# A two-layer attention kernel: new places in the queue of layer 1's epilogue, and own buffers for its last block

## The chip, the cores and the metric

The kernel runs on one core of a Trainium2 chip, in one launch. The metric is the device time of that launch in microseconds (us): from the first to the last instruction of the program. The kernel before takes 3108.49 us, the median of three runs that lie between 3106.8 and 3109.73 us. The profile and the trace quoted below are of one further execution whose span is 3106.2 us.

The core has five engines which run at the same time and wait for one another by semaphores. In the profile they are called PE (TensorE, the matrix multiplier), DVE (VectorE), ACT (ScalarE), POOL (GpSimd) and SP (SyncE, which here starts the DMA transfers). PEld is the loading of weights into PE, which overlaps its matmuls.

## The reference, cut to what matters

The input `x` is (4, 128, 64, 64): four images of 4096 positions with 128 channels, in float32. Two layers follow one another.

```python
# layer 0
x = x + L0_conv(gn(x), ...)          # group norm, q, k, v, gate; softmax attention of
                                     # 4096 x 4096 with 64 channels; gate; projection
# layer 1
t = to_tokens(x)
h = ln(t)                            # layer norm
q = h @ W
t = t + softmax(q @ q.T) @ h         # attention, 4096 x 4096, 128 channels
Wx = ln(t) @ Wf.T                    # inputs of a recurrence
Wx = batch_norm(Wx)                  # mean and variance over all 4 * 4096 tokens
y[s] = sigmoid(Wx[s] + y[s-1] @ V.T) # a recurrence along the 4096 tokens
out = from_tokens(t + y)
```

The batch norm is what makes the end of layer 1 matter: no step of the recurrence can start before the statistics of the very last block of the last image are known.

## The kernel before, as far as the change touches it

For each of the four images (`b`) the kernel runs `layer0` and then `layer1`. Each walks over eight blocks of 512 queries (`n`). Within a block the inner loop makes scores on PE, the exponential on ACT, sums or block transposes on DVE, and the weighted sum on PE again. One turn of this inner loop is called a *place* here. In every place at most one small closure is taken out of a queue: `pending` holds the epilogues of finished blocks, `ahead` the preparation of the next image. So the small steps lie between the large matmuls.

The queue in layer 0 (a place in each turn of the loop over `p`):

```python
        def nothing():
            pass
        ...
        def attention(score_mm, bias, scale, weigh, finish, need):
            ...
            for n in range(NB):
                for p in range(PAIRS):
                    ...                                   # scores (L215), exp (L217), acc (L224),
                                                          # weighted sums (L394)
                    if ahead:
                        ahead.popleft()()
                    elif pending and (p % 2 == 0 or len(pending) > 6):
                        pending.popleft()()
```

The epilogue of a block in layer 1. All four steps that use a PSUM bank take it from one pool that has a single buffer, `ps_m`; that pool also serves the preparation of the next image (`mp`, lines 326, 346 and 361).

```python
            def finish(n):
                ...
                t = work.tile([P, 4, NQ, 32], F32, tag="t", name="t1", bufs=2)
                h2 = work.tile([P, NQ, C], F32, tag="h2", name="h2")
                th = work.tile([P, QB], F32, tag="th", name="th")
                t1 = work.tile([P, NQ, C], F32, tag="og", name="t1b")
                nc.sync.dma_start(t, t_d[b, n])

                def tokens():
                    ...                                        # denominators
                    m = ps_m.tile([P, NQ, P], F32, tag="m", name="mt")
                    for j in range(NQ):
                        nc.tensor.transpose(m[:, j, :], oacc[:, n, bass.ts(j, P)], ident)  # L557
                    for j in range(NQ):
                        nc.vector.scalar_tensor_tensor(t1..., m..., rinv..., t...)         # L559
                    layernorm(quarters(t1), quarters(h2))      # DVE L267 L268, POOL L131 L132, DVE L271

                def result():
                    m = ps_m.tile([P, QB], F32, tag="m", name="mr")
                    ...                                        # 4 transposes of t1, L569
                    t2 = work.tile([P, QB], F32, tag="xb", name="t2")
                    nc.scalar.copy(t2, m)                      # L571
                    nc.sync.dma_start(t2_d[b, :, cs], t2)      # L572

                def turn():
                    m = ps_m.tile([P, QB], F32, tag="m", name="mh")
                    ...                                        # 4 transposes of h2, L577
                    nc.scalar.copy(th, m)                      # L578

                def inputs():
                    m = ps_m.tile([P, QB], F32, tag="m", name="mw")
                    nc.tensor.matmul(m, lhsT=wt["f"], rhs=th, start=True, stop=True)       # L582
                    nc.vector.bn_stats(bn_st[:, b * NB + n, :], m)                         # L583
                    ...                                        # copy to wxs, L586 (wx, L589)

                if b == B - 1 and n == 0:
                    pending.extend([tokens, turn, inputs, result])
                else:
                    pending.extend([tokens, result, turn, inputs])
```

In layer 1 a place takes from `pending` first and from `ahead` only when `pending` is empty:

```python
                        if pending:
                            pending.popleft()()
                        elif ahead:
                            ahead.popleft()()
```

The end of layer 1 and the start of the recurrence:

```python
        flush()                                    # what is left in pending
        ok = big.tile(...)                         # checks of the denominators
        ...
    with ExitStack() as st:
        scan = st.enter_context(tc.tile_pool(name="scan", bufs=1))
        ...
        banks = ...                                # six banks, each begun by one matmul, L725
        mv = scan.tile([P, 2], F32, name="bn_mv")
        nc.vector.bn_aggr(mv, bn_st...)            # L730
        gain = scan.tile([P, 1], F32, name="gain")
        inv_sqrt(gain, mv[:, 1:2], EPS_BN)         # POOL L131 L132
        ...                                        # gain and bias, L737
        preload(1); preload(2)                     # L751
        for k, i in enumerate(steps):              # 44 steps, in two halves each
            ...
                if k == 0:
                    nc.scalar.activation(dst, at(wxs, i, bs), AF.Sigmoid, ...)   # L761
                    continue
                nc.tensor.matmul(bank(k, s), lhsT=wt["vt"], rhs=before, ...)     # L764
                nc.scalar.activation(dst, bank(k, s), AF.Sigmoid, bias=bias)     # L768
```

The program that is run is not in the order of this text: each engine's instructions are put in order when the program is built. An engine then takes them one after the other.

Of the kernel before, what the change touches and what calls it, by code (L numbers as in the profile page):

```python
# [10 lines left out]
F32 = mybir.dt.float32  # L11
I32 = mybir.dt.int32
AF = mybir.ActivationFunctionType
# [5 lines left out]
P = 128  # L19
B, C, N = 4, 128, 4096  # L20
# [9 lines left out]
QB = 512  # L30
NB = N // QB
NQ = QB // P
# [125 lines left out]
def fast(  # L158
# [3 lines left out]
    nc = tc.nc  # L162
    keep_ctx = ExitStack()
    keep = keep_ctx.enter_context(tc.tile_pool(name="keep", bufs=1))
    bn_st = keep.tile([P, B * NB, 6], F32, name="bn_st")
    den_all = keep.tile([P, 2 * B * NT], F32, name="den_all")

    with ExitStack() as st:
        big = st.enter_context(tc.tile_pool(name="big", bufs=1))
        ep = st.enter_context(tc.tile_pool(name="ep", bufs=4))  # L170
        accp = st.enter_context(tc.tile_pool(name="accp", bufs=1))
        work = st.enter_context(tc.tile_pool(name="work", bufs=1))
        stat = st.enter_context(tc.tile_pool(name="stat", bufs=4))
        ps_s = st.enter_context(tc.tile_pool(name="ps_s", bufs=2, space=PSUM))
        ps_o = st.enter_context(tc.tile_pool(name="ps_o", bufs=3, space=PSUM))
        ps_m = st.enter_context(tc.tile_pool(name="ps_m", bufs=1, space=PSUM))
# [4 lines left out]
        pending: deque = deque()  # L181

        def nothing():
            pass

        done = set()

# [5 lines left out]
        def attention(score_mm, bias, scale, weigh, finish, need):  # L193


            fifo: deque = deque()
            o = None

            def pop():
                nonlocal o  # L200
                n, p, e, acc = fifo.popleft()
                if p == 0:
                    o = None
                o = weigh(o, n, p, e)
                if p == PAIRS - 1:
                    finish(n, o, acc)

            for n in range(NB):
                acc = first = None
                for p in range(PAIRS):  # L210
                    need(n, p)
                    ps = ps_s.tile([P, 2, QB], F32, tag="s", name="ps")
                    for h in range(2):
                        lhsT, rhs = score_mm(n, p, h)
                        nc.tensor.matmul(ps[:, h, :], lhsT=lhsT, rhs=rhs, start=True, stop=True)  # L215
                    e = ep.tile([P, 2, QB], F32, tag="e", name="e")
                    nc.scalar.activation(e, ps, AF.Exp, scale=scale)  # L217
                    if p == 0:
                        first = e
                    elif p == 1:  # L220
                        acc = accp.tile([P, 2, QB], F32, tag="acc", name="acc", bufs=2)
                        nc.vector.tensor_tensor(acc, first, e, ALU.add)
                    else:
                        nc.vector.tensor_tensor(acc, acc, e, ALU.add)  # L224
                    fifo.append((n, p, e, acc))
                    if len(fifo) > LAG:
                        pop()
                        if p == 0:
                            pop()
                    if ahead:  # L230
                        ahead.popleft()()
                    elif pending and (p % 2 == 0 or len(pending) > 6):
                        pending.popleft()()
            while fifo:
                pop()
# [25 lines left out]
        def layernorm(src, dst):  # L261

            mv = stat.tile([P, NQ, 2], F32, tag="mv", name="mv")
            rstd = stat.tile([P, NQ], F32, tag="rstd", name="rstd")
            for j in range(NQ):
                s6 = stat.tile([P, 6], F32, tag="s6", name="s6")
                nc.vector.bn_stats(s6, src[j])  # L267
                nc.vector.bn_aggr(mv[:, j, :], s6)  # L268
            inv_sqrt(rstd, mv[:, :, 1], EPS_LN)
            for j in range(NQ):  # L270
                nc.vector.tensor_scalar(  # L271
                    dst[j], src[j], mv[:, j, 0:1], rstd[:, j : j + 1],
                    ALU.subtract, ALU.mult,
                )
# [191 lines left out]
        def layer1(b, h, qt):  # L466
# [74 lines left out]
            def finish(n):  # L541
                cs = bass.ts(n, QB)
                rinv = stat.tile([P, NQ], F32, tag="rinv", name="rinv")
                t = work.tile([P, 4, NQ, 32], F32, tag="t", name="t1", bufs=2)
                h2 = work.tile([P, NQ, C], F32, tag="h2", name="h2")
                th = work.tile([P, QB], F32, tag="th", name="th")
                t1 = work.tile([P, NQ, C], F32, tag="og", name="t1b")
                nc.sync.dma_start(t, t_d[b, n])

                def tokens():  # L550
                    at = (B + b) * NT + n * NQ
                    den = den_all[:, at : at + NQ]
                    nc.vector.tensor_reduce(den, slots[:, bass.ts(n, NQ), :], AX.X, ALU.add)
                    nc.vector.reciprocal(rinv, den)
                    m = ps_m.tile([P, NQ, P], F32, tag="m", name="mt")
                    for j in range(NQ):
                        nc.tensor.transpose(m[:, j, :], oacc[:, n, bass.ts(j, P)], ident)  # L557
                    for j in range(NQ):
                        nc.vector.scalar_tensor_tensor(  # L559
                            t1[:, j, :].rearrange("q (p i) -> q p i", p=4),  # L560
                            m[:, j, :].rearrange("q (p i) -> q p i", p=4), rinv[:, j : j + 1],
                            t[:, :, j, :], ALU.mult, ALU.add,
                        )
                    layernorm(quarters(t1), quarters(h2))

                def result():
                    m = ps_m.tile([P, QB], F32, tag="m", name="mr")
                    for j in range(NQ):
                        nc.tensor.transpose(m[:, bass.ts(j, P)], t1[:, j, :], ident)  # L569
                    t2 = work.tile([P, QB], F32, tag="xb", name="t2")  # L570
                    nc.scalar.copy(t2, m)  # L571
                    nc.sync.dma_start(t2_d[b, :, cs], t2)  # L572

                def turn():
                    m = ps_m.tile([P, QB], F32, tag="m", name="mh")
                    for j in range(NQ):
                        nc.tensor.transpose(m[:, bass.ts(j, P)], h2[:, j, :], ident)  # L577
                    nc.scalar.copy(th, m)  # L578

                def inputs():  # L580
                    m = ps_m.tile([P, QB], F32, tag="m", name="mw")
                    nc.tensor.matmul(m, lhsT=wt["f"], rhs=th, start=True, stop=True)  # L582
                    nc.vector.bn_stats(bn_st[:, b * NB + n, :], m)  # L583
                    m = m.rearrange("p (g i s) -> p i g s", i=L // 2, s=2)
                    if b == B - 1:
                        nc.vector.tensor_copy(wxs[:, :, b, bass.ts(n, GB), :], m)  # L586
                    else:
                        wx = work.tile([P, L // 2, GB, 2], F32, tag="wx", name="wx")
                        nc.vector.tensor_copy(wx, m)  # L589
                        nc.sync.dma_start(wxs_d[b, :, :, bass.ts(n, GB), :], wx)  # L590

                if b == B - 1 and n == 0:
                    pending.extend([tokens, turn, inputs, result])
                else:
                    pending.extend([tokens, result, turn, inputs])


            for n in [NB - 2, NB - 1] + list(range(NB - 3, -1, -1)):
# [4 lines left out]
                for a in order(n):  # L603
# [4 lines left out]
                    for i in range(2):  # L608
                        ps = ps_s.tile([P, 2, QB], F32, tag="s", name="ps")
                        e = ep.tile([P, 2, QB], F32, tag="e", name="e")  # L610
# [68 lines left out]
        def need(n, p):  # L679

            if n == 0:
                while p // 4 > 0 and n_ahead - len(ahead) < 6 * (p // 4):
                    ahead.popleft()()

        for b in range(B):
            xg, q, k, v = parts0
# [13 lines left out]
                ahead.popleft()()  # L700
        flush()

        ok = big.tile([P, 2, 2 * B * NT], F32, tag="oacc", name="ok")
        nc.vector.tensor_scalar(ok[:, 0, :], den_all, DEN_LO, None, ALU.is_ge)
        nc.vector.tensor_scalar(ok[:, 1, :], den_all, DEN_HI, None, ALU.is_le)
# [3 lines left out]
    with ExitStack() as st:  # L709
        scan = st.enter_context(tc.tile_pool(name="scan", bufs=1))  # L710
        ps_r = st.enter_context(tc.tile_pool(name="ps_r", bufs=1, space=PSUM))
        t2 = scan.tile([P, B, N], F32, name="t2s")
# [10 lines left out]
        for s in range(2):  # L723
            for i in range(3):
# [1 line left out]
                    banks[s][i][:, : HB * G], lhsT=ident, rhs=wxs[:, 0, :HB, :, 0],  # L726
                    start=True, stop=True, skip_group_check=True,
                )
        mv = scan.tile([P, 2], F32, name="bn_mv")
        nc.vector.bn_aggr(mv, bn_st.rearrange("p a b -> p (a b)"))  # L730
        gain = scan.tile([P, 1], F32, name="gain")
        inv_sqrt(gain, mv[:, 1:2], EPS_BN)
        nc.vector.tensor_mul(gain, gain, col(GAMMA))

        bias = scan.tile([P, 1], F32, name="bias")
        nc.vector.tensor_mul(bias, mv[:, 0:1], gain)
        nc.vector.tensor_sub(bias, col(BETA), bias)  # L737

# [3 lines left out]
        def bank(k, s):  # L742
            return banks[s][k % 3][:, : HB * G].rearrange("p (b g) -> p b g", g=G)
# [12 lines left out]
        for k, i in enumerate(steps):  # L756
# [15 lines left out]
            if k >= W:  # L772
                todo.extend((i - 3, b) for b in range(B) if i % 4 == 3)
                for j in range(len(todo) if i == L - 1 else min(1, len(todo))):
                    i0, b = todo.popleft()
# [418 lines left out]
```

## Time and profile before

| what | before |
|---|---|
| median of the runs | 3108.49 us |
| span of the profiled execution | 3106.2 us |
| PE busy | 3018.6 us, 97% of the span |
| DVE busy | 1877.7 us, 60% |
| ACT busy | 1144.8 us, 37% |
| POOL busy | 144.5 us, 5% |
| mean granted PE clock | 0.993 |

The first table of the profile's page says how long each engine was busy. The list of waits says, for each pair of an instruction and the one that it waited for, how many us the waiting engine sat idle in total, how many times, and how long at most. The timeline gives instructions in order of time: start in us, duration in us, engine, line, operation, the tile written, an arrow to the tiles read, and in square brackets the idle time of that engine just before, with the instruction that ended it. A table by windows cuts the span into stretches and gives each engine's busy time in each. A float32 matmul of this kernel stands in the trace as two records.

### The profile page before, as it was taken

Reading aid. Unit: us, or ns where it says so; the run is one execution under the profiler, and the core shown is the slowest. Engines: PE = TensorE matmul, PEld = TensorE weight load, DVE = VectorE, ACT = ScalarE, POOL = GpSimd, SP = SyncE. Lnnn points to the kernel's source line nnn. Section 1 sums busy time; section 2 is a strip of 40 time slices with the busy share of each in tenths; the row PEclk is TensorE's granted clock in tenths of the full one; section 3 lists DMA queues with packets and bytes.
Section 4 is the critical chain, followed back from the end, with each engine's and each line's share of the span. In section 5 each row is a group of like instructions: output and inputs, shape, how many; then the busy total and the mean of one; then the engine's idle time right before and its main releaser. Section 6 shows DMA issues by size and latency. Waiting matters only on the chain.

```text
span 3106.2 us, 32252 instructions
## 1 busy us (share of the span) xinstructions
PE 3018.6 (97%) x10706; PEld 1362.3 (44%) x10706; DVE 1877.7 (60%) x3160; ACT 1144.8 (37%) x2018; POOL 144.5 (5%) x183
## 2 busy tenths in 40 slices
PE   7999999999999999999999999999999999999976
PEld 3444444444444444444444444444444444444432
DVE  6666656555666665655566666555566666455546
ACT  3444433333344443333334443333334444323324
POOL 0000000000000000000000000000000000000000
PEclk9999999999999999999999999999999999999988
DMA  1011143333111123334211114333321113443423
GB/s 51 28 55 55 55 111 88 91 89 92 46 55 55 55 78 93 90 89 97 73 52 55 50 43 116 88 91 93 91 56 55 49 44 121 114 104 88 98 98 157
DMA packets 233168, 241.14 MB, mean 78 GB/s; under 512 B 88480, under 2 KB 144288, under 8 KB 231968
## 3 DMA queue, kind: packets, MB, share of 16 engines
q1 hardware_dynamic: 231984, 238.18, 28.2%
q8 instruction: 88, 1.44, 0.2%
q10 hardware_dynamic: 1008, 0.79, 0.1%
q14 instruction: 88, 0.72, 0.1%
HBM read 65.80 MB, written 56.62 MB: 39 GB/s over the span
## 4 chain that ended last, share of the span: by engine, by line
PE 91%; DVE 4%; SPq 1%; POOL 1%; DMA 1%; issue 1%; ACT 0%; ACTq 0%; DVEq 0%; POOLq 0%
PE o L394 28%; PE ps L215 15%; PE ps L613 15%; PE o L501 14%; PE ot L514 12%; SPq L650 1%; PE m L243 1%; PE mw L582 1%; PE mq L487 1%; PE mp L326 1%; PE ps_r L764 1%; PE mh L577 1%; POOL rstd L132 1%; DVE t1b L559 1%; PE mp L361 1%; PE mp L346 1%
## 5 line engine op out<-in xcount | busy, mean ns | idle before, releaser
L394 PE MATMUL o<-e,nxt 64*128 64x512 f32 x4096 | 963.8, 589 | 0.0
L217 ACT ACTIVATE e<-ps 128x1024 f32<-128x1024 f32 x512 | 521.4, 1025 | 674.7 <-PE ps L215 657.5
L224 DVE TENSOR_TENSOR acc<-acc,e 128x1024 f32<-128x1024 f32 x448 | 547.6, 1222 | 236.4 <-ACT e L217 220.5
L619 ACT ACTIVATE e<-ps,shift 128x512 f32<-128x512 f32 x580 | 393.9, 684 | 749.8 <-PE ps L613 497.1
L394 PEld LDWEIGHTS o<-e,nxt 64*128 64x128 f32 x4096 | 399.0, 187 | 482.3 <-issue 474.5
L613 PE MATMUL ps<-qt 128*128 128x512 f32 x1160 | 547.8, 595 | 2.7 <-ACT qt L488 2.7
L501 PE MATMUL o<-e,h 128*128 128x512 f32 x1160 | 537.7, 592 | 0.0
L215 PE MATMUL ps<-nxt 64*128 64x512 f32 x2048 | 534.5, 596 | 1.2 <-DVE nxt L338 0.9
L514 PE MATMUL ot<-tt,h 128*128 128x512 f32 x888 | 399.8, 593 | 0.0
L624 DVE STREAM_TRANSPOSE dd<-e 128x512 f32<-128x512 f32 x444 | 286.5, 686 | 83.4 <-ACT e L619 73.1
L501 PEld LDWEIGHTS o<-e,h 128*128 128x128 f32 x1160 | 218.3, 191 | 260.7 <-issue 259.5
L613 PEld LDWEIGHTS ps<-qt 128*128 128x128 f32 x1160 | 213.4, 191 | 249.0 <-issue 224.2
L215 PEld LDWEIGHTS ps<-nxt 64*128 64x128 f32 x2048 | 194.5, 187 | 231.5 <-issue 158.8
L514 PEld LDWEIGHTS ot<-tt,h 128*128 128x128 f32 x888 | 167.9, 190 | 210.0 <-issue 205.7
L519 DVE TENSOR_REDUCE slots<-tt 128x4 f32<-128x2048 f32 x111 | 250.7, 2258 | 9.7 <-DMA tt<-dd 9.4
L528 DVE TENSOR_TENSOR oacc<-oacc,ot 128x512 f32<-128x512 f32 x87 | 59.3, 682 | 209.8 <-PE ot L514 209.8
L131 POOL TENSOR_SCALAR rstd<-mv 128x4 f32<-128x4 f32 x64 | 14.6, 228 | 2456.5 <-DVE mv L268 2456.5
L619 ACT ACTIVATION_READ_ACCUMULATOR e<-ps,shift 128x1 f32 x580 | 113.9, 196 | 0.0
L448 DVE SCALAR_TENSOR_TENSOR t<-yt,rinv,t 128x128 f32<-128x128 f32 x128 | 36.6, 347 | 71.5 <-DMA yt<-turn_d 71.4
L411 POOL TENSOR_SCALAR xb<-xb,bpc 128x512 f32<-128x512 f32 x32 | 57.4, 1793 | 318.0 <-DMA xb<-in_x_dram 289.3
L132 POOL TENSOR_TENSOR rstd<-rstd,mhalf 128x4 f32<-128x4 f32 x64 | 66.4, 1038 | 5.3
L271 DVE TENSOR_SCALAR h<-t,mv,rstd 128x128 f32<-128x128 f32 x128 | 35.7, 343 | 47.1 <-POOL rstd L132 47.1
(134 smaller groups left out, 1491.7 us busy)
## 6 DMA issues: line engine op xcount, KB each, us to landing
tt<-dd SPq DMA_DIRECT2D x1776, 64.0 KB, 2.0
turn_d<-d SPq DMA_DIRECT2D x96, 256.0 KB, 2.0
t_d<-t SPq DMA_DIRECT2D x64, 256.0 KB, 2.0
nxt<-in_x_dram SPq DMA_DIRECT2D x16, 512.0 KB, 5.5
xb<-in_x_dram SPq DMA_DIRECT2D x32, 256.0 KB, 2.9
t<-turn_d SPq DMA_DIRECT2D x128, 64.0 KB, 2.0
yt<-turn_d SPq DMA_DIRECT2D x128, 64.0 KB, 2.0
qt<-turn_d SPq DMA_DIRECT2D x128, 64.0 KB, 2.0
```

Of the source, the lines that this page charges most:

```text
L132: nc.gpsimd.tensor_tensor(dst, dst, mhalf[:, :n], ALU.pow)
L215: nc.tensor.matmul(ps[:, h, :], lhsT=lhsT, rhs=rhs, start=True, stop=True)
L217: nc.scalar.activation(e, ps, AF.Exp, scale=scale)
L224: nc.vector.tensor_tensor(acc, acc, e, ALU.add)
L394: nc.tensor.matmul(o[r], lhsT=v[rs, p + h * PAIRS, :], rhs=e[rs, h, :], start=(p == 0 and h == 0), stop=(p == PAIRS - 1 and h == 1),)
L501: nc.tensor.matmul(o, lhsT=h[:, NQ * a + 2 * i + half, :], rhs=e[:, half, :], start=(a == order(n)[0] and i == 0 and half == 0), stop=(a = ...
L514: nc.tensor.matmul(ot, lhsT=h[:, NQ * n + j, :], rhs=t[:, :, j, :, :].rearrange("q p k j -> q k p j"), start=(j == 0), stop=(j == NQ - 1),)
L519: nc.vector.tensor_reduce(slots[:, bass.ts(n, NQ), a], t.rearrange("q p b k j -> q b p (k j)"), AX.XY, ALU.add,)
L528: nc.vector.tensor_tensor(oacc[:, n, :], oacc[:, n, :], o, ALU.add)
L613: nc.tensor.matmul(ps[:, half, :], lhsT=qt[:, bass.ts(at, P)], rhs=qt[:, bass.ts(n, QB)], start=True, stop=True,)
L619: nc.scalar.activation(e[:, half, :], ps[:, half, :], AF.Exp, bias=shift, accum_out=slots[:, at, n : n + 1],)
L624: nc.vector.transpose(d.rearrange("q f b k j -> q k b f j")[:, 2 * i + half], e[:, half, :].rearrange("q (b f j) -> q b f j", b=NQ, f=NQ),)
```

## The change

The change has five parts, all of them about the place and the buffers of small steps; no arithmetic is added or left out, except for one activation on a single column.

1. In layer 1 two places called `nothing` come between `result` and `turn`, so that the layer norm of `tokens` has more time before PE needs it. In such a place one step of `ahead` is taken, if there is one. In the last image the blocks 1, 2 and 3 are without them.
2. In layer 0 the entries that `pending` held at the start are taken in every place rather than in every second one.
3. The last block of the last image takes its PSUM banks from the pool of the scores and its SBUF buffers from the pool of the exponentials; its `tokens` step goes to the front of the queue.
4. The statistics and the gain and bias of the batch norm move from the pool of the recurrence to one that lives from the start.
5. A Sigmoid on one column is written after the last block, to have that function's table loaded early.

```diff
+    mv = keep.tile([P, 2], F32, name="bn_mv")
+    gain = keep.tile([P, 1], F32, name="gain")
+    bias = keep.tile([P, 1], F32, name="bias")
+    first_y = keep.tile([P, 1], F32, name="first_y")
 ...
         def nothing():
-            pass
+            if ahead:
+                ahead.popleft()()
 ...
+            left = len(pending)
 ...
-                    elif pending and (p % 2 == 0 or len(pending) > 6):
+                    elif pending and (p % 2 == 0 or left > 0 or len(pending) > 6):
+                        left -= 1
                         pending.popleft()()
 ...
+                if b == B - 1 and n == 0:
+                    one, two = (ep.tile([P, 2, QB], F32, tag="e", name="last") for _ in range(2))
+                    h2, t1 = (one[:, r, :].rearrange("q (j c) -> q j c", j=NQ) for r in range(2))
+                    th, t2 = two[:, 0, :], two[:, 1, :]
+                    def bank():
+                        return ps_s.tile([P, 2, QB], F32, tag="s", name="ml")[:, 0, :]
+                else:
+                    ...                            # buffers as before, bank() from ps_m
 ...
                 if b == B - 1 and n == 0:
-                    pending.extend([tokens, turn, inputs, result])
+                    pending.appendleft(tokens)
+                    pending.extend([result, turn, inputs])
+                elif b == B - 1 and n < 4:
+                    pending.extend([tokens, result, turn, inputs])
                 else:
-                    pending.extend([tokens, result, turn, inputs])
+                    pending.extend([tokens, result, nothing, nothing, turn, inputs])
 ...
         flush()
+        nc.scalar.activation(first_y, shift, AF.Sigmoid)
 ...
-        mv = scan.tile([P, 2], F32, name="bn_mv")
-        gain = scan.tile([P, 1], F32, name="gain")
-        bias = scan.tile([P, 1], F32, name="bias")
```

## The prediction

> **What bounds the kernel now.** I read the first table of the page, then the list of PE's waits, then the timeline around these waits, and last the table by windows.
>
> ```profile
> PE 3018.6 (97%) x10706; PEld 1362.3 (44%) x10706; DVE 1877.7 (60%) x3160; ACT 1144.8 (37%) x2018; POOL 144.5 (5%) x183
> ```
>
> PE is busy for all but 88 us of the 3106.2. The change takes no matmul away, so it can only win from those 88 us and from the few places where PE runs at half its clock. That alone says that 2% (62 us) is out of reach. Where are the 88 us, and which of them does the change touch? The list of waits, PE's own (total us, times, longest):
>
> ```profile
> PE mh L577 <- DVE h L271: 15.7, 21, 4.4
> PE ps_r L764 <- ACT y L761: 7.8, 1, 7.8
> ...
> PE mh L577 <- ACT e L619: 2.8, 3, 1.0
> ...
> PE mp L346 <- DVE nxt L351: 2.4, 3, 0.8
> PE mp L326 <- DVE nxt L351: 2.4, 3, 0.8
> ```
>
> The reader is to see three kinds: `turn` waiting for the layer norm (`mh`), two projections of the next image waiting for their single bank (`mp`), and waits that occur once, around the start of the recurrence (`ps_r`). One of the 24 `mh` waits, the longest, belongs to the last kind. A usual one looks like this in the timeline:
>
> ```profile
> 652.79 1.12 DVE L559 SCALAR_TENSOR_TENSOR t1b<-mt,rinv,t 128x128 f32<-128x128 f32 x4
> ...
> 655.97 1.04 POOL L132 TENSOR_TENSOR rstd<-rstd,mhalf 128x4 f32<-128x4 f32 x1
> ...
> 657.04 1.11 DVE L271 TENSOR_SCALAR h<-t1b,mv,rstd 128x128 f32<-128x128 f32 x4 [1.47 <-POOL rstd L132]
> ...
> 657.53 0.75 PE L577 MATMUL mh<-ident,h 128*128 128x128 f32 x3 [0.65 <-DVE h L271]
> ```
>
> Four DVE steps, the statistics, a round trip to POOL and four more DVE steps take 5.4 us (652.79 to 658.15); PE comes 0.65 us early. And the end of layer 1:
>
> ```profile
> 2996.32 0.68 DVE L528 TENSOR_TENSOR oacc<-oacc,o 128x512 f32<-128x512 f32 x1
> ...
> 3001.45 0.66 PE L557 MATMUL mt<-ident,oacc 128*128 128x128 f32 x4
> ...
> 3006.01 1.11 DVE L271 TENSOR_SCALAR h<-t1b,mv,rstd 128x128 f32<-128x128 f32 x4 [0.58 <-POOL rstd L132]
> ...
> 3008.38 2.08 PE L582 MATMUL mw<-th,w 128*128 128x512 f32 x2 [0.73 <-ACT th L578]
> ...
> 3011.11 0.67 DVE L586 COPY wxs<-mw 128x512 f32<-128x512 f32 x1
> ...
> 3015.81 1.02 DVE L730 BATCH_NORM_AGGREGATE bn_mv<-bn_st 128x2 f32<-128x192 f32 x1 [4.03 <-DMA t_d<-t]
> ...
> 3018.81 1.28 ACT L761 ACT_TABLE_LOAD   x1 [5.24 <-DVE bias L737]
> ...
> 3020.77 15.27 PE L764 MATMUL ps_r<-y,w 128*128 128x256 f32 x44 [7.82 <-ACT y L761]
> ```
>
> The last sum is there at 2997.00, but its transposes start at 3001.45, behind the other block's three uses of the one bank. The batch statistics are there at 3011.19, but the aggregate starts at 3015.81: its tile lies where a buffer was whose DMA had to land first. From 2997.00 to the first matmul of the recurrence it takes 23.8 us. The table by windows (length, then PE, PEld, DVE, ACT, POOL busy, PE's clock, DMA):
>
> ```profile
> 2997.00:3020.00 23.00, 9.36 (x32) 5.14 (x32) 10.07 (x33) 2.95 (x4) 2.18 (x5) 0.72 0.20 67
> ```
>
> PE's mean clock here is 0.72; the trace's clock record has it at half from 3006.9 to 3024.0.
>
> **What the Trainium skill says.** "TensorE: Matmul & The Clock Gate", section "What's actually happening": PE falls to half rate after about one idle window of 3.4 us and comes back after one busy window. The trace agrees: PE sat idle for 4.39 us before 3006.50, the clock fell at 3006.9, and the two records of `mw`, 1.11 us in all a block earlier (at 2998.96), took 2.08. [...] "PSUM — Partial Sum Buffer", "Engine vs sequencer instructions": matmuls start in program order and the other engines' queues are first in, first out. The timeline agrees: PE starts nothing else while `mh` waits. So where an instruction stands in its engine's queue decides, and that is known from the built program before any run.
>
> **The change, part by part.**
>
> *Two empty places.* In the built order of the first three images, `mh` comes two to four score records (one or two score matmuls) later than before, with weighted sums besides, in the six blocks per image that still lie in layer 1; the place of `h` in DVE's queue is as before. In layer 0 PE did not wait for `mh`, so the other two blocks have nothing to win. Two score records alone are 2 x 0.43 = 0.86 us and the sums between them bring more, against waits of 0.39 to 0.95 us. So these waits go. Per image they are 0.39 + 0.65 + 0.65 + 0.39 + 0.65 + 0.95 = 3.67 us. A matmul record lasts 590 ns, yet in a stream the next starts after 429, so each stall also loses the overlap of 0.16: 3.67 + 6 x 0.16 = 4.63, times three is **13.9 us**. In the last image blocks 7 and 6 move in the order; 5, 4 and 2 do not. That is (0.39 + 0.65) + 2 x 0.16 = **1.4 us** won; 2.1 us of waits stay.
>
> *`nothing` takes a step of `ahead`.* This spreads the preparation of the next image. In the order before, once per later image, two value projections and one query/key projection stand back to back on the one bank; in the new order other matmuls are between. That removes both `mp` waits: (0.78 + 0.17) x 2 x 3 = **5.7 us**, where 0.17 is again the lost overlap (276 ns record, 112 step). Against it, in three places a gate projection now stands only one matmul (0.86 us) ahead of `mh` on the same bank, and ACT's 0.78 us read with some 0.2 us before it must fit between: I allow **1.0 us** lost in all.
>
> *Leftovers in every place of layer 0.* More entries are left over than before, six per block instead of four. In the windows of layer 0 DVE is busy 229 of 343 us and PE all of it, so DVE has room and PE's matmuls only change their place: **0**.
>
> *The last block.* Its `mt` can start at 2997.06 rather than 3001.45. Its layer norm meets one obstacle: in DVE's new order the `bn_stats` of block 1 stands ahead of the last aggregate of the last block, and waits for `mw` of block 1, which ended at 3000.07. So `bn_stats` runs until about 3000.7, and from the last aggregate to `h` it was 3006.01 - 3004.35 = 1.66 us: `h` at 3002.4. From `h` to `mw` as before, 2.37: 3004.75. `mw` at full clock 1.11: 3005.9. Statistics and copy, 1.3: 3007.2. The tile of the aggregate has its own place now, so it starts at once: 3007.2 against 3015.81, **8.6 us** earlier. If the clock falls all the same, `mw` takes its 2.08 and it is 7.6. With full clock the first two steps of the recurrence also take about 2.6 instead of 3.6 us, 1.0 more. The six matmuls that begin the banks, which stood in idle time, now come after that last copy: 12 x 0.227 = 2.7 us, twice that at half clock. From the copy to the first matmul of the recurrence there are about 5 us, so they cost nothing at full and 0.5 at half clock. So 7.1 to 9.6; I take **8.8**.
>
> *The early table.* In the built order this activation stands at the very start of ACT's queue, since it needs only a constant. The table for the recurrence is still loaded after the bias: nothing won of the 1.28. At the start there is one load more, and ACT sits idle 14.4 us before its first activation and 2.3 before its first exponential: **0**, give or take 1.
>
> Sum: 13.9 + 1.4 + 5.7 - 1.0 + 8.8 = 28.8 us. 3108.5 - 28.8 = 3079.7, so 3080.
>
> **Rivals.**
> 1. *The wait only moves.* `mh` could come later and meet another wait: for the bank, for ACT's copy, or for a later `h` if DVE is late. For it: one bank serves five kinds of steps. Against it: `h` keeps its place, and in layer 0 with its longer distance no `mh` waited. If the waits of the empty places came back in full, 3095.
> 2. *The leftovers crowd layer 0.* Steps with 4 us of DVE work next to 1.22 us per place could hold back DVE, then the four buffers of the exponentials, then PE. For it: a place of layer 0 lasts only 2.6 us. Against it: the old rule also took one in every place while more than six were left, and PE shows no wait there. A few us per image, 3085 to 3095.
> 3. *The end is bound elsewhere.* If the recurrence's first tile must wait for memory of the last block's buffers, as the aggregate had to, part of the 8.8 is given back. Against it: the result's copy and DMA now stand ahead of `turn`, and a DMA landed in about 2 us before. It would make 3083 to 3085.
>
> **Range and chances.** The waits found are nearly certain to be at hand and the order says that they are passed, so most of the risk is in small new waits (later) and in the clock (2 us either way). Range 3073 to 3091: the low end needs all parts at their best and some further waits of the 88 us gone, the high end is one rival half true. Faster by over 2% would need 62 us: 0.01. Slower by over 2%: 0.01.
>
> **What would show it.** Right: no `mh` waits on `h` in the first three images, three left in the last; no waits of `mp` for L351's counterpart in layer 1; the aggregate directly after the copy of the last inputs, some 10 us after the last sum; a table load still between bias and recurrence, and three loads in all. Wrong: new waits of PE in the first blocks of layer 0 or at `mh` for ACT, or an aggregate that waits for a DMA still.

## The result and the profile after

The changed kernel takes **3074.59 us** (median of four runs, 3073.29 to 3075.83) against 3107.64 in the same comparison: ratio 0.9893, 95% interval 0.9875 to 0.9910. That is 33.1 us, against 28.8 foretold. In the profiled executions the spans are 3106.2 and 3074.0 us.

The first table of the page, after:

```profile
PE 3009.1 (98%) x10706; PEld 1366.4 (44%) x10706; DVE 1878.9 (61%) x3160; ACT 1144.4 (37%) x2020; POOL 149.3 (5%) x183
```

The counts say that no matmul went away; ACT has two instructions more, the early Sigmoid and its table load. PE's busy time fell by 9.5 us although it does the same work. That fits what the profile counts as busy: in a stream the record of a matmul (590 ns) overlaps the next one (429 ns later), before a stall it does not, and a group that waits piece by piece counts as busy throughout.

The lines of the changed kernel are numbered otherwise: the last epilogue's steps are L579 (`mt`), L592 (`mr`), L601 (`mh`) and L606 (`mw`), the scores of layer 1 L640, those of layer 0 L223. The list of PE's waits after, in the parts that answer to those shown of before (total, times, longest):

```profile
PE ps L640 <- ACT qt L497: 2.7, 4, 0.7
PE ml L601 <- DVE last L280: 2.5, 1, 2.5
PE ps L223 <- ACT e L225: 2.2, 1, 2.2
PE m L601 <- DVE h L280: 2.1, 3, 0.8
```

The waits of the projections (`mp`) are gone, and of the waits for the layer norm three are left, 2.1 us, all in the last image. One is new: a score of layer 0 waits 2.2 us for ACT. The end in the timeline:

```profile
2973.29 0.68 DVE L537 TENSOR_TENSOR oacc<-oacc,o 128x512 f32<-128x512 f32 x1
...
2974.02 0.65 PE L579 MATMUL ml<-ident,oacc 128*128 128x128 f32 x4 [1.66 <-DVE oacc L537]
...
2979.26 1.11 DVE L280 TENSOR_SCALAR last<-last,mv,rstd 128x128 f32<-128x128 f32 x4 [0.90 <-POOL rstd L132]
...
2981.43 1.56 PE L606 MATMUL ml<-last,w 128*128 128x512 f32 x2 [0.68 <-ACT last L602]
...
2983.64 0.68 DVE L610 COPY wxs<-ml 128x512 f32<-128x512 f32 x1
2984.23 1.01 DVE L758 BATCH_NORM_AGGREGATE bn_mv<-bn_st 128x2 f32<-128x192 f32 x1
...
2984.46 5.00 PE L754 MATMUL ps_r<-wxs,ident 128*128 128x256 f32 x12 [1.47 <-DVE wxs L610]
...
2987.22 1.28 ACT L787 ACT_TABLE_LOAD   x1 [5.84 <-DVE bias L763]
...
2989.30 6.08 PE L790 MATMUL ps_r<-y,w 128*128 128x256 f32 x19
```

The transposes of the last block follow its last sum at once, the aggregate follows the copy at once, and the table load still stands between bias and recurrence.

Dividing both traces at the first score matmul of each layer, at the end of the last sum and at the first matmul of the recurrence gives the account of the 32.1 us between the spans:

| stage | before, us | after, us | difference | foretold |
|---|---|---|---|---|
| start to layer 1 of image 1 | 393.29 | 396.73 | +3.4 | 0, give or take 1 |
| layer 1, each of images 1 to 3 | 391.0 | 381.9 | -9.2 | |
| layer 0 after it | 351.5 | 352.3, last 353.0 | +0.8, last +1.5 | |
| the two together, three times | 2227.5 | 2203.1 | -24.4 | -18.6 |
| layer 1 of image 4 to the last sum | 376.2 | 374.1 | -2.1 | -1.4 |
| last sum to the first matmul of the recurrence | 23.8 | 15.3 | -8.4 | -8.6 |
| recurrence to the end | 85.4 | 84.7 | -0.7 | -1.0 at best |

The 0.7 us that the last layer 0 takes beyond the others stand in e1 too (353.0), but not in e2 (352.3); no run explains them.

So the forecast is near for a mixed reason: the end was right to a fraction of a us, the middle won 5.8 us more than foretold, and the start lost 3.4 that I had written down as hidden. The experiments are about these two, and about what bounds the end now.

### The profile page after: what moved, and what is told of

Read it like the earlier page. It is cut to its first block, busy times and chain, and to the rows that moved or that the text cites. A ratio compares the mean times of both kernels' runs of the same rounds, so it can differ in the third digit from the quotient of the medians.

```text
span 3074.0 us, 32253 instructions
## 1 busy us (share of the span) xinstructions
PE 3009.1 (98%) x10706; PEld 1366.4 (44%) x10706; DVE 1878.9 (61%) x3160; ACT 1144.4 (37%) x2020; POOL 149.3 (5%) x183
## 4 chain that ended last, share of the span: by engine, by line
PE 95%; DVE 2%; DMA 1%; ACT 1%; POOL 0%; issue 0%; SPq 0%; ACTq 0%; DVEq 0%; POOLq 0%
PE o L403 28%; PE ps L640 16%; PE o L510 16%; PE ps L223 14%; PE ot L523 12%; PE m L252 1%; PE m L606 1%; PE mq L496 1%; PE mp L335 1%; PE mp L355 1%; PE mp L370 1%; DVE t2s L804 1%; DVE ps_r L777 1%; PE m L601 1%; PE ps_r L790 0%; PE m L579 0%
## 5 line engine op out<-in xcount | busy, mean ns | idle before, releaser
L225 ACT ACTIVATE e<-ps 128x1024 f32<-128x1024 f32 x512 | 521.7, 1025 | 679.4 <-PE ps L223 647.3
L640 PE MATMUL ps<-qt 128*128 128x512 f32 x1160 | 547.6, 594 | 2.7 <-ACT qt L497 2.7
L223 PE MATMUL ps<-nxt 64*128 64x512 f32 x2048 | 535.3, 597 | 2.6 <-ACT e L225 2.2
L640 PEld LDWEIGHTS ps<-qt 128*128 128x128 f32 x1160 | 213.5, 190 | 247.4 <-issue 224.1
L223 PEld LDWEIGHTS ps<-nxt 64*128 64x128 f32 x2048 | 194.3, 187 | 232.2 <-issue 157.9
L528 DVE TENSOR_REDUCE slots<-tt 128x4 f32<-128x2048 f32 x111 | 250.6, 2258 | 10.2 <-DMA tt<-dd 7.4
```

The source lines that it names most:

```text
L528: nc.vector.tensor_reduce(slots[:, bass.ts(n, NQ), a], t.rearrange("q p b k j -> q b p (k j)"), AX.XY, ALU.add,)
L640: nc.tensor.matmul(ps[:, half, :], lhsT=qt[:, bass.ts(at, P)], rhs=qt[:, bass.ts(n, QB)], start=True, stop=True,)
```

## The experiments

All runs are compared with the kernel before on the same chip; its medians lay between 3106.79 and 3107.95 us.

### e1 and e2: the early Sigmoid

e1 leaves the Sigmoid out:

```diff
-        nc.scalar.activation(first_y, shift, AF.Sigmoid)
```

> The changed kernel without the Sigmoid on one column, nothing else. In the changed kernel the first image reached layer 1 at 396.7 us, 3.4 later than before (393.3). Theory: the Sigmoid, which went to the start of ACT's queue, costs these 3.4 us (one more table load of 1.28 in front of the first exponential, a later second tanh, and half a clock from 32.9 to 36.3 us), and wins nothing at the end, so without it layer 1 starts at 393.3 again and the kernel takes 3074.6 - 3.4 = 3071.2 us. Rival: only the load of 1.28 us counts, the rest is the phase of the clock: 3073.3, layer 1 at 395.4. Second rival: the Sigmoid is hidden at the start and the loss comes from elsewhere: 3074.6 and 396.7.

3072.96 us (3071.27 to 3073.77), ratio 0.9884 (0.9867 to 0.9900). From the first score to layer 1 it takes 365.96 us as before the change, where the changed kernel takes 369.23: the start's loss is the Sigmoid's. What it did there is seen in the timeline of the changed kernel:

```profile
26.26 1.67 DVE L347 TENSOR_SCALAR nxt<-pp,par 64x512 f32<-64x512 f32 x2
...
28.42 0.69 DVE L360 TENSOR_TENSOR nxt<-po,bc 128x512 f32<-128x512 f32 x1
...
29.14 0.63 ACT L364 ACTIVATE nxt<-nxt 128x512 f32<-128x512 f32 x1 [2.26 <-DVE nxt L360]
...
29.79 1.28 ACT L225 ACT_TABLE_LOAD   x1
...
31.09 1.94 ACT L225 ACTIVATE e<-ps 128x1024 f32<-128x1024 f32 x2
...
32.16 1.42 PE L223 MATMUL ps<-nxt 64*128 64x512 f32 x4 [2.20 <-ACT e L225]
...
33.37 3.34 PE L403 MATMUL o<-e,nxt 64*128 64x512 f32 x8
```

and in that of the kernel before:

```profile
25.73 0.68 DVE L351 TENSOR_TENSOR nxt<-po,bc 128x512 f32<-128x512 f32 x1
...
26.45 1.68 DVE L338 TENSOR_SCALAR nxt<-pp,par 64x512 f32<-64x512 f32 x2
...
26.45 0.63 ACT L355 ACTIVATE nxt<-nxt 128x512 f32<-128x512 f32 x1 [0.42 <-DVE nxt L351]
...
29.34 1.02 ACT L217 ACTIVATE e<-ps 128x1024 f32<-128x1024 f32 x1 [2.26 <-PE ps L215]
...
30.42 1.13 PE L215 MATMUL ps<-nxt 64*128 64x512 f32 x4 [0.26 <-ACT e L217]
...
31.38 1.88 PE L394 MATMUL o<-e,nxt 64*128 64x512 f32 x8
```

The first exponential (L225, before L217) is 1.75 us later. ACT's second Tanh (L364, before L355) moved to 29.14 from 26.45: DVE's order changed with the new instruction, so that the sum which this Tanh reads (L360, before L351) now comes after the two scalings (L347, before L338) and not ahead of them. Behind the Tanh stands a table load that was not there: the load for the Sigmoid is at 7.07, the Tanh after it needs none, and the exponential does. PE waits 2.2 us instead of 0.26. From 32.88 to 36.29 PE's clock is at half, so the eight matmul records after that wait take 3.34 instead of 1.88 us. Of the changed kernel this is one execution; whether the half clock at the start comes in each one is not shown.

The medians differ by only 1.6 us, and the ranges of the two kernels overlap. In the profiled executions it is 2.0: the start is 3.3 us shorter, the first score came 0.5 us later, and the end was longer by 0.9, from the last sum to the recurrence 16.3 instead of 15.3. There the clock was at half for 10.2 us rather than 6.8. e2 keeps the Sigmoid but lets it read a number that is only known near the end:

```diff
-        nc.scalar.activation(first_y, shift, AF.Sigmoid)
+        nc.scalar.activation(first_y, bn_st[:, (B - 1) * NB + 1, 0:1], AF.Sigmoid)
```

> The changed kernel with the Sigmoid reading a column of the batch statistics of the last image's block 1, so that it cannot be put at the start. Theory: the table is now loaded while ACT waits for the last layer norm, and 1.28 us go from the path between the bias and the recurrence, besides the 3.4 us at the start: 3074.6 - 3.4 - 1.3 = 3069.9 us; from the copy of the last inputs to the first matmul of the recurrence 3.7 instead of 5.0 us. Rival: the six matmuls that begin the banks, 5 us at half clock, now bound that stretch: it stays near 5.0 and the time at 3071.2.

3072.02 us (3070.93 to 3072.16), ratio 0.9881 (0.9865 to 0.9898). The rival was right for the end: the load has gone from the path, yet the stretch from the copy to the recurrence is 5.4 us. The timeline of e2:

```profile
2977.39 2.07 PE L606 MATMUL ml<-last,w 128*128 128x512 f32 x2 [0.67 <-ACT last L602]
...
2980.93 5.46 PE L754 MATMUL ps_r<-wxs,ident 128*128 128x256 f32 x12 [1.47 <-DVE wxs L610]
...
2983.72 1.14 ACT L787 ACTIVATE y<-wxs,bias,gain 128x256 f32<-128x256 f32 x2 [6.38 <-DVE bias L763]
...
2986.19 2.10 PE L790 MATMUL ps_r<-y,w 128*128 128x256 f32 x5
```

The first Sigmoid of the recurrence starts at 2983.72, but PE is still at the six matmuls that begin the banks, which at half clock take 5.5 us.

### e5: the same end with PE kept busy

```diff
+                def warm():
+                    m = bank()
+                    for _ in range(2):
+                        nc.tensor.matmul(m, lhsT=wt["f"], rhs=qt[:, :QB], start=True, stop=True)
-                    pending.extend([result, turn, inputs])
+                    pending.extend([result, warm, turn, inputs])
```

> e2 with two more matmuls (w_f by 512 columns of qt into a bank that nobody reads) between result and turn of the last block; they are additional work whose product is not used. In e2 PE sat idle 2.5 us there, its clock fell to half at 2976.8 us, mw took 2.07 us and the six matmuls that begin the banks 5.3, so that the first matmul of the recurrence waited for PE and not for the table: 5.4 us after the copy of the last inputs. Theory: half a clock, not the number of matmuls, holds back the end. With the gap filled the clock stays full, mw takes 1.1, the banks 2.7 and the stretch from copy to recurrence falls to some 3.7: 2.7 us less than e2, 3069.3. Rival: the clock falls all the same, because the rest of the window is too idle, and the two matmuls only stand in the way: 3072 to 3073.

**3070.39 us** (3069.94 to 3071.16), ratio 0.9879 (0.9863 to 0.9896), the fastest of all; every one of its runs lies below every run of the changed kernel. Its timeline:

```profile
2973.81 2.54 PE L619 MATMUL ml<-qt,w 128*128 128x512 f32 x4
...
2978.05 1.13 PE L606 MATMUL ml<-last,w 128*128 128x512 f32 x2 [0.68 <-ACT last L602]
...
2980.65 2.96 PE L759 MATMUL ps_r<-wxs,ident 128*128 128x256 f32 x12 [1.47 <-DVE wxs L610]
...
2984.10 0.72 PE L795 MATMUL ps_r<-y,w 128*128 128x256 f32 x2 [0.49 <-ACT y L792]
```

`mw` takes 1.13 and the banks 2.96 us, and from the copy (2980.50) to the recurrence it is 3.6 us, as foretold: the half clock held back the end. It won 1.6 rather than 2.7 us, since the clock did not stay full as I had said: it fell once, earlier, from 2971.7 to 2975.1, and block 1's `mw` and statistics, which stand ahead of the last aggregate of the last block on DVE, came about 0.9 us later. e6 below ends as e2 does, without these two matmuls; in its execution the clock came back at 2985.05, while the banks were at work, and it is 4.6 us from the copy to the recurrence. So the end follows the clock. That it was the two matmuls which kept the clock up is read from one execution of e5, and the intervals of e5 and e2 overlap.

### e3, e4 and e10: what the two places do

e3 is the kernel before with the places and the leftover rule alone, `[tokens, result, nothing, nothing, turn, inputs]` with `nothing` taking a step of `ahead`.

> The kernel before with parts 1 and 2 of the change alone: the two places, which take a step of the next image's preparation, and the leftovers in every place; the end as before. Theory: layer 1 of each of the first three images takes 381.9 instead of 391.0 us and layer 0 after it 352.3 instead of 351.5, so 8.4 per image, and 2.0 in the last image: 3107.6 - 25.1 - 2.0 = 3080.5 us. Rival: the buffers of the last block also take part in this gain (the scores' pool, the tail of the last image): under 22 us.

3080.29 us (3079.38 to 3080.48), ratio 0.9908 (0.9892 to 0.9925). The theory holds to 0.2 us: the middle's gain is that of the places. In e4 the places stay empty:

```diff
         def nothing():
-            if ahead:
-                ahead.popleft()()
+            pass
```

> As e3, but the two places stay empty; they take no step of the next image's preparation. Theory: the waits of the transposes for the layer norm (6.5 us per image with what they lose inside the group of four) go as in e3, but the two waits of the projections for their one bank (1.9 us per image) stay or move, since it was the earlier start of the preparation that spread them: layer 1 at 383.8 us, in all about 5.8 slower than e3, 3086. Rival: the spreading is the work of the later turn of the transposes alone, and e4 is as fast as e3; or the preparation doesn't fit any more and is done at the end of layer 1, with PE waiting: some 10 us per image slower than e3.

3099.13 us (3097.77 to 3101.82), ratio 0.9973 (0.9962 to 0.9985): 18.8 us slower than e3, three times what I had expected. PE's waits in e4:

```profile
PE ps L617 <- ACT e L623: 2.4, 3, 0.8
PE mp L348 <- DVE nxt L353: 2.4, 3, 0.8
PE mp L328 <- DVE nxt L353: 2.3, 3, 0.8
```

Both waits of the projections are back, as foretold, and the waits for the layer norm stay away from the first three images. But the second rival was right too, in kind: four gate projections (L363) per image no longer fit into layer 1. They are done at the border, between the first scores of the next layer 0:

```profile
774.50 1.02 PE L363 MATMUL mp<-nxt,w 128*128 128x512 f32 x2
775.46 1.12 PE L216 MATMUL ps<-nxt 64*128 64x512 f32 x2
776.51 1.12 PE L363 MATMUL mp<-nxt,w 128*128 128x512 f32 x2
```

In e3 the same scores stand together:

```profile
775.25 1.99 PE L217 MATMUL ps<-nxt 64*128 64x512 f32 x8
```

Eight records, which are four matmuls, take 1.99 us where they stand side by side; one matmul of two records between others takes 1.05 us to the next start, as long as two matmuls side by side in the same trace (779.67 to 780.73). These matmuls use half of the rows each, and by these times two of them run at once only if no other stands between. Layer 0 after it takes 358.2 instead of 352.3 us, while layer 1 takes 381.8, as in e3. Summed from each start to the next, of these 5.9 us per image 2.0 come from the waits for the bank, 0.9 from the scores of layer 1, which now wait once for ACT, and 2.2 from the border: the four projections take 4.2 us there, 0.9 more than in layer 1, and the scores 1.3 more. So a place that is really empty gives back two thirds of what it wins; that `nothing` takes a step is what makes the places pay.

e10 is e2 with one place in place of two.

> e2 with one place instead of two between result and turn. In the built order mh now stands at most one score record later than in the kernel before, in some blocks not at all, while the projections of the next image are spread as in e2. Theory: the two gains of the places are separate; the waits for the bank (1.9 us per image) are gone, of the waits for the layer norm (6.5 us per image in all) about half stays: layer 1 of the first three images at some 385 us instead of 381.9, the kernel at 3081. Rival: one more closure is margin enough, since the waits are under 1 us: 382 and 3072.

3079.47 us (3077.65 to 3080.40), ratio 0.9907 (0.9891 to 0.9924), 7.5 slower than e2. Its waits:

```profile
PE m L601 <- DVE h L280: 6.2, 11, 0.8
```

Eleven waits for the layer norm, of which each of the first three images has two (0.65 and 0.39 us) and the last image five; none of `mp`. Layer 1 takes 383.8 us: the gain at the bank stays, and 2.0 of the gain at the layer norm goes. I had said half; it is a third of 6.3. The two gains are separate, and two places are needed.

### e6 and e7: the leftover rule and the last image

e6 is e2 with the old rule `elif pending and (p % 2 == 0 or len(pending) > 6)`.

> e2 with the old rule for leftovers in layer 0 (every second place once six or fewer are left), that is, without part 2 of the change. Theory: PE is the bound in layer 0 and its matmuls only change their place, so layer 0 of images 2 to 4 takes 352.3 us as with the new rule, and the kernel 3072.0. Rival: part 2 is needed because the leftovers would push the first epilogue of layer 0 and let PE wait: layer 0 some us longer per image.

3072.01 us (3071.25 to 3073.83), ratio 0.9885 (0.9868 to 0.9901): as e2, but partly by luck. Layer 0 takes 352.8 instead of 352.3 us, with a wait of 0.27 at its first scores, so part 2 is worth about half a us per image, 1.6 in all. In the profiled execution these came back elsewhere: the first score came 1.0 us sooner, and the end took 15.4 instead of 16.3 us with the clock at half for 6.8 rather than 10.2. e7 is e2 with `n < 2` for `n < 4`, so that blocks 3 and 2 of the last image have their places too.

> e2 with the two places also for blocks 3 and 2 of the last image. Theory: the wait of 0.8 us of block 2 goes, but the queue is longer when the last sum comes, so that block 1's turn and inputs come after those of the last block, and the aggregate waits for block 1: the stretch from the last sum to the recurrence grows from 16.3 to about 19 us, the kernel is at 3074. Rival: the last block goes first all the same, the end stays, and 0.8 us are won: 3071.

3073.98 us (3072.26 to 3074.33), ratio 0.9891 (0.9875 to 0.9908): not faster than e2. Block 2's wait is gone, and as I had said block 1 comes after the last block and the aggregate waits for its copy; from the last sum to the recurrence it takes 20.1 instead of 16.3 us. But the last sum comes 4.0 us sooner, as less is done ahead of it. From the start of the last layer 1 to the recurrence it takes 390.3 us, as in e2 (390.4): neither the 3 us lost nor the 0.8 won. What the 2 us between the medians are is not settled; the profiled spans are 3070.5 and 3070.4.

### e8 and e9: the end alone

e8 is the kernel before with parts 3 and 4 and no Sigmoid.

> The kernel before with parts 3 and 4 alone: the last block's own banks and buffers and its tokens first, the batch statistics in the lasting pool; no places, no early Sigmoid. Theory: the end from the last sum is as in the changed kernel, 15.3 to 16.3 us from the last sum to the recurrence instead of 23.8, and the rest as before: 3107.7 - 8.5 = 3099 us. Rival: the end gains by the places in the last image as well, then less than 7 us here.

3098.64 us (3096.93 to 3101.98), ratio 0.9974 (0.9961 to 0.9986). From the last sum to the recurrence 16.4 us. With e3 this closes the account: 8.2 from the end and 27.4 from the places make 35.6; less the 3.4 of the Sigmoid, 32.2, where the change has 33.1. What the last block's own bank, its own buffers, its place in the queue and the earlier DMA of its result give each is not taken apart. e9 moves the batch statistics alone:

```diff
+    mv = keep.tile([P, 2], F32, name="bn_mv")      # gain and bias likewise
-        mv = scan.tile([P, 2], F32, name="bn_mv")
```

> The kernel before with part 4 alone: mean, variance, gain and bias of the batch norm in the lasting pool. Theory: the aggregate no longer waits 4.0 us for the DMA of the last result and starts after the copy of the last inputs at once: 3107.7 - 4.0 = 3103.7 us. Rival: the first tile of the recurrence lies in the memory which that DMA reads, and waits instead: the aggregate starts early, but the first Sigmoid of the recurrence still comes 7.5 us after the last result's copy, and nothing is won.

3104.55 us (3103.25 to 3108.82), ratio 0.9994 (0.9987 to 1.0001), which is not clear of the measurement. The timeline tells why it is less than 4 us:

```profile
3010.66 1.01 DVE L732 BATCH_NORM_AGGREGATE bn_mv<-bn_st 128x2 f32<-128x192 f32 x1
...
3014.70 0.11 POOL L720 MEMSET state<- 128x4 f32 x1 [2.06 <-DMA t_d<-t]
3014.73 1.28 ACT L761 ACT_TABLE_LOAD   x1 [2.19 <-DVE ps_r L751]
```

The aggregate starts 4 us earlier, with the copy's end, but the table load in front of the first Sigmoid starts only at 3014.73, when the DMA of the last result has landed (the line of `state` shows the landing; its memory is from the same pool). The trace names a DVE instruction as the releaser of the load, yet the bias had been there since 3013.5. The trace also has ACT's waits on semaphores ahead of the load: the one for the semaphore of the last result's DMA stood from 3012.03 to 3014.55, and that DMA landed at 3014.52. So it is the same wait. From copy to recurrence it is 6.0 us instead of 9.0: 3.0 of the 4.0 us are won, and the rest of the wait turns up again a few instructions later. In the changed kernel the result's DMA goes out before `turn`, and there the stretch is 5.0.

## Why the prediction was right or wrong, point by point

- **PE bounds, and the order decides: right.** All 23 usual waits were named, and after the change those are gone that the order said would go. The three of the last image that stayed were foretold as well. But that the change could win only from the 88 us of idle time and from half clock was wrong: 9.5 us came out of PE's busy time. Nor do 88 us of idle time put 62 us out of reach by themselves.
- **The waits at the layer norm, 13.9 us: right mechanism, size too small.** Summing the time from each PE record's start to the next one's in layer 1 of an image, by line, scores lose 2.0 us, weighted sums 3.0, `mh` 1.1 (after taking off the four records that moved to layer 0, 0.6 us) and `mw` 0.2: 6.3 per image, not 4.63. The term that was too small is what each wait costs beyond its idle time, put at 0.16 us and measured at (6.3 - 3.67) / 6 = 0.44. The two waits of the last image that went gave 2.1 us for the same reason, not 1.4. `h` comes in four pieces, one from each of four DVE instructions 0.26 us apart, and each of the four transposes waits for its own. A group that met `h` in the making, before, and one that found it ready, after:

```profile
712.38 1.01 PE L577 MATMUL mh<-ident,h 128*128 128x128 f32 x4 [0.39 <-DVE h L271]
```

```profile
660.11 0.66 PE L601 MATMUL m<-ident,h 128*128 128x128 f32 x4
```

  The 0.35 us inside the group stands in no idle time of the list of waits, as PE counts as busy.
- **The waits at the bank, 5.7 us: right.** The value projections lose 1.92 us per image, 5.8 in all, and e10 shows this gain without most of the other.
- **1.0 us lost to the gates: wrong.** The wait that I feared is 0.011 us in each of the three places, so ACT had read the bank in time.
- **Leftovers, 0: right within a us per image.** The layer 0 stages are 0.8 us longer, of which 0.6 is one block's four transposes that moved there from layer 1.
- **The last block, 8.8: right.** `h` began 5.3 us after the last sum (5.4 foretold), the copy's end 10.35 (10.2), the recurrence 4.98 after that (about 5). But I took the clock to hold more than not, and it fell at 2982.0: the banks took 5.0 instead of 2.7 us and only just ended in time. The end's gain with the recurrence is 9.1.
- **The early table, "0, give or take 1": the step that failed.** That it would win nothing was right. That it would be hidden was not: the added load stands behind the second Tanh, in front of the first exponential. I counted ACT's idle time there as room for it, though the second Tanh fills that room as soon as it comes later, and did not look at DVE's order, which the added instruction changed. It cost 3.3 us from the first score to layer 1: without the Sigmoid at the start, in e1 and e2, the stretch takes 365.96 us as before.

The two largest errors, 5.8 us more in the middle and 3.4 lost at the start, partly cancel, and that is luck: the figure was better than the reasons for the start.

## What to carry to other kernels

When an in-order engine waits for a chain on other engines, count the places between request and use in the built order, and fill added places with work that has to be done anyway: an empty place pushed other work to the border of the stages, and gave back 18.8 of 27.4 us. An instruction meant to load a table late had to read something that exists only late; reading a constant, it was put at the start, where it cost 3.3 us. And a wait list shows idle time only: a group that waits piece by piece looks busy.

## What the runs showed of the hardware that was not expected

I had taken from the Trainium skill, "TensorE: Matmul & The Clock Gate", section "What's actually happening", that the clock falls after an idle window of 3.4 us, and so took it to hold more than not in the new end, whose longest gap is 2.5 us. The traces do not fit a window that is idle throughout. Tables by windows of 3.4 us, laid so that they end where the clock's changes in the record fall (PE busy is the figure after the length, PE's clock the fraction behind POOL's); the changed kernel:

```profile
2971.75:2975.17 3.42, 1.75 (x14) 1.26 (x12) 2.16 (x7) 0.59 (x1) 0.47 (x1) 1.00 0.20 77
2975.17:2978.58 3.41, 1.88 (x6) 0.80 (x6) 3.02 (x13) 1.17 (x2) 0.62 (x2) 1.00 0.00 0
2978.58:2981.99 3.41, 1.66 (x6) 0.85 (x6) 2.20 (x7) 0.59 (x1) 0.64 (x1) 1.00 0.20 77
2981.99:2985.40 3.41, 1.94 (x4) 0.83 (x3) 2.22 (x3) 0.00 (x0) 0.17 (x2) 0.50 0.47 111
```

the kernel before:

```profile
3000.10:3003.52 3.42, 1.98 (x10) 1.17 (x8) 2.66 (x8) 0.00 (x0) 0.00 (x0) 1.00 0.01 2
3003.52:3006.93 3.41, 0.43 (x3) 0.29 (x3) 2.80 (x14) 0.00 (x0) 1.27 (x2) 1.00 0.00 0
```

and e5:

```profile
2968.30:2971.70 3.40, 1.79 (x11) 1.24 (x12) 2.65 (x10) 1.07 (x2) 0.00 (x0) 1.00 0.20 77
2971.70:2975.10 3.40, 3.40 (x6) 1.65 (x7) 2.24 (x10) 1.03 (x2) 0.52 (x2) 0.50 0.00 0
```

After windows with PE busy for 1.98, 1.88 and 1.75 us the clock stayed; after 1.79, 1.66 and 0.43 it fell. So a window that is about half idle was enough in some cases, and the busy time of the profile, whose ends are modelled, gives no clean limit: 1.75 stayed and 1.79 fell. The first fall in the end comes 8.0 us after the last sum in the changed kernel and 6.9 in e1, which has the same end. That the windows lie differently from run to run would explain why one had 6.8 us at half clock and the other 10.2; no run sets it apart.
